# Experts' gates and ups as stationary operands, and VectorE steps with one operand from SBUF, in a linear-attention and mixture-of-experts layer

## The chip, the cores and the metric

The kernel runs on one core of a Trainium2 chip. The metric is the device time of one execution in microseconds (us). Matrix products run on TensorE (PE in the profile, its weight loads PEld); element-wise work runs on VectorE (DVE), ScalarE (ACT) and GpSimd (POOL). SyncE (SP) issues most transfers, POOL those that are indexed by row. Products land in PSUM; the kernel keeps everything else on the chip in SBUF.

## What is computed

A block on x of 4 batches x 1024 tokens x 256 channels, everything in fp32: x + attention(norm(x)) + experts(norm(x)).

```python
# attention, 16 heads of 16 channels
sq, sk = elu(q) + 1, elu(k) + 1
coarse = (sq @ M) / clip(sq @ z)                     # M, z: sums over 4 memories
fine   = sum_m softmax(mean n_f)[m] * (sq @ M_m) / clip(sq @ z_m)
prob   = sigmoid(relu(coarse @ eg_w1.T + eg_b1) @ eg_w2.T + eg_b2)
memory = prob * fine + (1 - prob) * coarse
local  = causal_linear_attention(q, k, v, chunk=128)
out    = (gate * memory + (1 - gate) * local) @ w_o.T
# experts: 8, of 176 inner channels, the best two of each token; one shared expert of 352
g = silu(x @ w_gate[e].T) * (x @ w_up[e].T)
y = sum_e cw[:, e] * (g @ w_down[e].T) + shared(x)
```

## The kernel before

**Stages.** The 4096 tokens are 32 tiles of 128. A first stage (to about 50 us) normalizes all of them, writes the normalized rows to a buffer `xns` in HBM and computes the values and the router's logits. Then the tokens are sorted by expert into 71 tiles of 128 slots, each tile with rows of one expert alone. From about 90 us on come 32 rounds, counted from 0, one for each token tile, and a tail. Each round does the attention of its token tile; rounds 2 to 29 also take a share of the projections, of the shared expert and of the 71 expert tiles. All is issued in an order written out by hand: every step is a unit with a weight, and `mix` merges the lists of a round in proportion to these weights. Each engine works through its own instructions in that order, and waits on semaphores where it needs another engine.

**A round of attention** (`attention_round`). `scores` (line 723) writes four masks' worth of products into the PSUM tile `quad`; VectorE masks them (`sT`, line 730). `turned(n-1)` (line 892) transposes `o` of the tile before, together with `coarse`. `output` multiplies it with `w_o` (`po`, lines 990 and 994). `memory` (line 838) reuses `quad`, once the masks have read it. `weigh` makes `rw` and `coarse` on VectorE (lines 848 to 853) and `cg` on POOL (line 860). `gate_hidden` forms the product `ph`, and VectorE adds the bias and reduces it to `z` (lines 917 and 919). `fine` makes `fm` in two VectorE steps (line 867); POOL makes `diff` of it in three steps (lines 878, 881, 882). `local` multiplies the masked scores with the values (`pn`, line 749). `gate_out(n-1)` makes `prob` on ScalarE and VectorE (lines 925 and 926) and `o = diff * prob + base` on VectorE (line 928). `back` (lines 765 and 771) forms `pb` in PSUM; VectorE makes `rden` of its denominators (lines 779 to 781) and `loc` (line 783). POOL adds `cg` to `loc` (line 789), which is `base` for the next round's `gate_out`. `loc` has one buffer. `update` adds to the running state (lines 818, 824, 829).

**An expert tile j.** `fetch_rows` gathers 128 rows of `xns` (POOL, line 1038). `fetch_weights` reads the expert's gates and ups (`wgu`) and downs (`wdn`) on SP. `expert_turn` transposes the hidden rows of tile j and the gathered rows of tile j+2 into one bank `pte`, and ScalarE copies it to `turned` (line 1077). `expert_hidden` multiplies: the turned rows are stationary, 352 columns of gates and ups move through, and `phe` has tokens on the partitions. ScalarE takes a tanh (line 1089) and VectorE two steps (lines 1090 and 1091). `expert_out` multiplies the turned hidden rows with `wdn` in two halves of 88 channels (`pye`, line 1097), ScalarE weighs the result (line 1101), and `put` adds it to the rows of `sums` in HBM (POOL, line 1106).

**PSUM.** `quad` takes four of the eight banks. All other products of the rounds take turns on four banks (`ps_r`, made by `bank`), in the order in which they are issued.

Of the kernel before, what the change touches and what calls it, by code (L numbers as in the profile page):

```python
# [8 lines left out]
FP = mybir.dt.float32  # L9
I32 = mybir.dt.int32  # L10
AF = mybir.ActivationFunctionType
ALU = mybir.AluOpType
AX = mybir.AxisListType

P = 128
NT = 4
TB = P * NT
EPS = 1e-6
# [4 lines left out]
def linear_attention_moe_kernel(  # L23
# [28 lines left out]
    nc = tc.nc  # L52
    T, H = x.shape
    S = T // B
    NH = memory_gate.shape[1]
    HD = H // NH
    NC = H // P
    HC = NH // NC
    NG = HC // 2
    NM = memories.shape[1]  # L60
    D1 = HD + 1
    CW = 32
    FR = E * F
    FT = w_gate.shape[1]
    FS = FT - FR
    NF = -(-FS // P)
    FH = F // 2
    assert FH * 2 == F and FH <= P and NC == 2 and NM == 4
    HID = eg_w1.shape[1]
    NBLK = T // TB  # L70
    NTT = T // P

    NST = 2 * NTT + E - 1
# [7 lines left out]
    const = ctx.enter_context(tc.tile_pool(name="const", bufs=1))  # L81
    io = ctx.enter_context(tc.tile_pool(name="io", bufs=NBLK))
    att = ctx.enter_context(tc.tile_pool(name="att", bufs=2))
    tmp = ctx.enter_context(tc.tile_pool(name="tmp", bufs=2))
    small = ctx.enter_context(tc.tile_pool(name="small", bufs=2))
    big = ctx.enter_context(tc.tile_pool(name="big", bufs=NBLK + 1))
    exw = ctx.enter_context(tc.tile_pool(name="exw", bufs=3))
    exp = ctx.enter_context(tc.tile_pool(name="exp", bufs=2))
    dram = ctx.enter_context(tc.tile_pool(name="dram", bufs=1, space=bass.MemoryType.DRAM))
# [5 lines left out]
    st = {}  # L95
    def bank(name):
        return ps_r.tile([P, 512], FP, tag="r", name=name)
# [48 lines left out]
    b1 = const.tile([P, HID], FP, tag="b1", name="b1")  # L146
# [27 lines left out]

    xns = dram.tile([T + P, H], FP, tag="xns", name="xns")
    sums = dram.tile([T + P, H], FP, tag="sums", name="sums")
    ident = const.tile([P, P], FP, tag="ident", name="ident")
    make_identity(nc, ident)
    ones = const.tile([P, P], FP, tag="ones", name="ones")
# [5 lines left out]
    for e in range(E):  # L185
# [5 lines left out]
        base=0, pattern=[[1, P]], channel_multiplier=-1,  # L191
# [53 lines left out]
    normx = const.tile([P, NC, NM, HC], FP, tag="normx", name="normx")  # L245
    alive = const.tile([P, NMN], FP, tag="alive", name="alive")

    hidden = [const.tile([P, FH + P], FP, tag=f"hidden{k}", name=f"hidden{k}") for k in range(2)]
    for t in hidden:
        nc.gpsimd.memset(t[:, F:], 0.0)  # L250
    ungate = const.tile([P, NH], FP, tag="ungate", name="ungate")
    gates = const.tile([P, H], FP, tag="gates", name="gates")

# [505 lines left out]
    def back(n):  # L759
        nT = st.pop(("nT", n))  # L760
        nq = NH // 4
        pb = bank(f"pb_{n}").rearrange("p (q t) -> p q t", q=nq)

        for q in range(nq):
            nc.tensor.matmul(
                pb[:, q, :], nT[:, q, :], ident,
                start=(q == 0), stop=False, is_transpose=True, skip_group_check=True,
            )
        blk, i, tok = at(n)
        for c in range(NC):  # L770
            nc.tensor.matmul(
                pb[:, 2 * c : 2 * c + 2, :].rearrange("p q (r k) -> p (q r) k", k=CW)[:, :, :D1],
                st["sqT", blk][:, c, tok],
                states[n % 2][:, c],
                start=False, stop=(c == NC - 1), skip_group_check=True,
            )
        pn3 = pb.rearrange("p q (r k) -> p (q r) k", k=CW)
        rden = small.tile([P, NH], FP, tag="rden", name=f"rden_{n}")
        nc.vector.tensor_scalar(rden, pn3[:, :, HD], EPS, None, ALU.max)
        nc.vector.reciprocal(rden, rden)  # L780
        nc.vector.tensor_mul(rden, rden, ungate)
        loc = tmp.tile([P, H], FP, tag="loc", name=f"loc_{n}", bufs=1)
        nc.vector.tensor_mul(  # L783
            loc.rearrange("p (h k) -> p h k", k=HD),
            pn3[:, :, :HD],
            rden[:, :, None].to_broadcast([P, NH, HD]),
        )

        nc.gpsimd.tensor_add(loc, loc, st["cg", n])
        st["base", n] = loc  # L790
# [117 lines left out]
    def gate_hidden(n):  # L908

        cT = st.pop(("cT", n))  # L910
        ph = bank(f"ph_{n}")
        for c in range(NC):
            nc.tensor.matmul(
                ph[:, :HID], cT[:, c, :], w1[:, c, :], start=(c == 0), stop=(c == NC - 1)
            )
        h1 = tmp.tile([P, HID], FP, tag="h1", name=f"h1_{n}")
        nc.vector.tensor_add(h1, ph[:, :HID], b1)  # L917
        z = small.tile([P, 1], FP, tag="z", name=f"z_{n}")
        nc.vector.scalar_tensor_tensor(h1, h1, 0.0, w2, ALU.max, ALU.mult, accum_out=z)
        st["z", n] = z  # L920

    def gate_out(n):

        prob = small.tile([P, 1], FP, tag="prob", name=f"prob_{n}")
        nc.scalar.activation(prob, st.pop(("z", n)), AF.Tanh, bias=b2, scale=0.5)
        nc.vector.tensor_scalar(prob, prob, 0.5, 0.5, ALU.mult, ALU.add)  # L926
        o = tmp.tile([P, H], FP, tag="o", name=f"o_{n}", bufs=1)
        nc.vector.scalar_tensor_tensor(  # L928
            o, st.pop(("diff", n)), prob, st.pop(("base", n)), ALU.mult, ALU.add
        )  # L930
        st["o", n] = o


    def shared_gate(blk, f):
# [99 lines left out]
    def fetch_rows(j):  # L1034
        if j >= NST:
            return
        xg = exp.tile([P, H], FP, tag="xg", name=f"xg_{j}", bufs=3)
        nc.gpsimd.indirect_dma_start(  # L1038
            out=xg,
            out_offset=None,  # L1040
            in_=xns,
            in_offset=bass.IndirectOffsetOnAxis(ap=islot[:, j : j + 1], axis=0),
        )
        st["xg", j] = xg

    def fetch_weights(j):
        if j >= NST:
            return
        e = nc.sync.value_load(owner[0:1, j : j + 1], min_val=0, max_val=(E - 1) * F)
        wgu = exw.tile([P, NC, 2, F], FP, tag="wgu", name=f"wgu_{j}")  # L1050
        for g, w in enumerate((w_gate, w_up)):
            nc.sync.dma_start(
                wgu[:, :, g, :],
                w[:, bass.ds(e, F)].rearrange("(k p) f -> p k f", p=P),
            )
        wdn = exw.tile([FH, 2, H], FP, tag="wdn", name=f"wdn_{j}")
        nc.sync.dma_start(
            wdn, w_down[bass.ds(e, F), :].rearrange("(f p) h -> p f h", p=FH)
        )
        st["weights", j] = wgu, wdn  # L1060

    def expert_turn(j):


        fetch_rows(j + 4)
        fetch_weights(j + 3)
        pt = bank(f"pte_{j}").rearrange("p (f t) -> p f t", t=P)
        lo, hi = (0 if j >= 0 else 2), (4 if j + 2 < NST else 2)
        if j >= 0:
            for f in range(2):  # L1070
                nc.tensor.transpose(pt[:, f, :], hidden[j % 2][:, f * FH : f * FH + P], ident)  # L1071
        if j + 2 < NST:
            xg = st.pop(("xg", j + 2))
            for c in range(NC):
                nc.tensor.transpose(pt[:, 2 + c, :], xg[:, c * P : (c + 1) * P], ident)  # L1075
        dst = exp.tile([P, 4, P], FP, tag="turned", name=f"turned_{j}")
        nc.scalar.copy(dst[:, lo:hi], pt[:, lo:hi])  # L1077
        st["hTe", j], st["xgT", j + 2] = dst[:, 0:2], dst[:, 2:4]

    def expert_hidden(j):  # L1080
        xgT, wgu = st.pop(("xgT", j)), st["weights", j][0]
        ph = bank(f"phe_{j}")
        for k in range(NC):
            nc.tensor.matmul(  # L1084
                ph[:, : 2 * F], xgT[:, k, :], wgu[:, k].rearrange("p g f -> p (g f)"),
                start=(k == 0), stop=(k == NC - 1),
            )
        th = hidden[j % 2][:, :F]
        nc.scalar.activation(th, ph[:, :F], AF.Tanh, scale=0.5)  # L1089
        nc.vector.scalar_tensor_tensor(th, th, 1.0, ph[:, :F], ALU.add, ALU.mult)  # L1090
        nc.vector.scalar_tensor_tensor(th, th, 0.5, ph[:, F : 2 * F], ALU.mult, ALU.mult)

    def expert_out(j):
        hT, wdn = st.pop(("hTe", j)), st.pop(("weights", j))[1]
        py = bank(f"pye_{j}")
        for f in range(2):
            nc.tensor.matmul(  # L1097
                py[:, :H], hT[:FH, f, :], wdn[:, f, :], start=(f == 0), stop=(f == 1)
            )
        y = exp.tile([P, H], FP, tag="y", name=f"y_{j}", bufs=3)  # L1100
        nc.scalar.activation(y, py[:, :H], AF.Copy, scale=wslot[:, j : j + 1])  # L1101
        st["y", j] = y
# [102 lines left out]
        return u  # L1205

    def experts():
        units = [(3000, lambda: None), (256, expert_turn, -2), (256, expert_turn, -1)]
        for j in range(NST + 1):
            if j < NST:  # L1210
                units += [(704, expert_hidden, j)]
            units += [(64, put, j - 2)] if j > 1 else []
            units += [(512, expert_out, j - 1)] if j > 0 else []
            units += [(512, expert_turn, j)] if j < NST else []
        return units + [(64, put, NST - 1)]

    def split(units, parts):
# [41 lines left out]
    for blk in range(NBLK):  # L1259
        rows = slice(blk * TB, (blk + 1) * TB)  # L1260
        nc.sync.dma_start(sums[rows, :], x[rows, :])


    def sorting():
# [128 lines left out]
```

## Time and profile before

| | |
|---|---|
| median of 3 runs | 688.77 us (687.68 to 692.53) |
| the profiled execution | 687.07 us |
| its span, first to last instruction | 685.4 us |
| mean granted clock of TensorE | 0.99 |
| VectorE / ScalarE / POOL busy | 454.8 / 267.1 / 386.8 us |
| DMA | 81.52 MB, 119 GB/s in the mean |

A row of the costliest groups gives line, engine and operation, what is written and read, the shape, the count, then the busy time in us and the mean duration in ns, and last the idle time of the engine before them with what ended it. A row of the list of waits gives who waited for whom, us in total, how often, and the longest in us. A row of the timeline gives start and duration in us. Matmuls overlap each other, so that the time from one start to the next says what one costs, and a weight load overlaps the matmul before it. An fp32 product appears as two matmuls over the same columns, a transpose as one.

### The profile page before, as it was taken

How to read it: one execution, taken by the hardware profiler on the slowest of the kernel's cores; microseconds unless marked ns; L12 is line 12 of the kernel's file. 1: busy time of each engine (PE TensorE's matmuls, PEld its weight loads, DVE VectorE, ACT ScalarE, POOL GpSimd, SP SyncE). 2: the span in 40 equal slices, each digit the busy share in tenths (PEclk: the TensorE clock that was granted, in tenths of full speed). 3: DMA queues.
4: the chain of work that ended last, by engine and by line, in shares of the span. 5: the costliest groups of instructions: out<-in, count | busy, mean ns of one | idle time of the engine just before them, and what ended most of it. 6: DMA issues, size and time to landing. Idle time of an engine off the chain costs nothing.

```text
span 685.4 us, 14244 instructions
## 1 busy us (share of the span) xinstructions
PE 646.1 (94%) x5084; PEld 461.9 (67%) x5084; DVE 454.8 (66%) x1198; ACT 267.1 (39%) x614; POOL 386.8 (56%) x424
## 2 busy tenths in 40 slices
PE   4999999899999899999999999999898999999896
PEld 3874565677777666676776767677676776667475
DVE  6838997666666657565756666666676566777672
ACT  3754644334444343334433333334343444334210
POOL 4300254556776735565565555566666567686575
PEclk9999999999999989999999999999999999999999
DMA  9683000436565623344453433345556466563384
GB/s 302 216 279 93 0 1 2 119 91 160 119 145 127 141 64 84 91 100 94 95 103 88 98 95 92 83 112 125 120 124 142 102 145 139 127 149 75 80 282 154
DMA packets 86483, 81.52 MB, mean 119 GB/s; under 512 B 7549, under 2 KB 84013, under 8 KB 86285
## 3 DMA queue, kind: packets, MB, share of 16 engines
q1 hardware_dynamic: 71085, 60.40, 30.6%
q0 software_dynamic: 13632, 18.62, 16.0%
q10 hardware_dynamic: 1696, 1.58, 0.7%
q8 instruction: 41, 0.67, 0.4%
q14 instruction: 29, 0.24, 0.1%
HBM read 62.62 MB, written 22.15 MB: 124 GB/s over the span
## 4 chain that ended last, share of the span: by engine, by line
PE 78%; DVE 14%; ACT 3%; issue 2%; POOL 1%; DMA 1%; DVEq 0%; ACTq 0%
PE phe L1084 13%; PE pye L1097 9%; PE po L990 6%; PE quad L723 5%; PE psu L953 5%; PE pv L396 4%; PE pg L939 4%; PE pn L749 4%; PE po L994 4%; PE quad L838 4%; PE pk L632 3%; PE pq L632 3%; PE pte L1071 2%; PE pt L892 2%; PE pte L1075 2%
## 5 line engine op out<-in xcount | busy, mean ns | idle before, releaser
L1106 POOL DMA_INDIRECT sums<-y,islot x71 | 113.3, 1596 | 70.3 <-DMA sums<-y,islot 18.8
L1084 PE MATMUL phe<-wgu,turned 128*128 128x352 f32 x276 | 97.5, 476 | 3.0 <-ACT turned L1077 2.2
L1090 DVE SCALAR_TENSOR_TENSOR hidden<-hidden,phe 128x176 f32<-128x176 f32 x71 | 23.8, 335 | 95.5 <-ACT hidden L1089 94.9
L730 DVE TENSOR_TENSOR sT<-quad,causal 128x512 f32<-128x512 f32 x128 | 80.5, 683 | 7.5 <-PE quad L723 7.1
L1038 POOL DMA_INDIRECT xg<-xns,islot x71 | 70.5, 993 | 18.7 <-issue 10.8
L1097 PE MATMUL pye<-wdn,turned 88*128 88x256 f32 x284 | 76.7, 393 | 2.5 <-issue 2.4
L860 POOL TENSOR_TENSOR cg<-coarse,gates 128x256 f32<-128x256 f32 x32 | 24.5, 765 | 95.5 <-DVE h L917 59.0
L1084 PEld LDWEIGHTS phe<-wgu,turned 128*128 128x128 f32 x276 | 48.5, 192 | 25.8 <-issue 6.4
L1097 PEld LDWEIGHTS pye<-wdn,turned 88*128 88x128 f32 x284 | 49.8, 190 | 16.4 <-issue 9.9
L1101 ACT ACTIVATE y<-pye,wslot 128x256 f32<-128x256 f32 x71 | 33.6, 473 | 64.0 <-PE pye L1097 64.0
L878 POOL TENSOR_TENSOR fm<-fm 128x512 f32<-128x512 f32 x32 | 44.1, 1379 | 20.0 <-DVE fm L867 12.4
L1077 ACT COPY turned<-pte 128x512 f32<-128x512 f32 (+1 forms) x71 | 41.1, 578 | 34.2 <-PE pte L1075 32.0
L1089 ACT ACTIVATE hidden<-phe 128x176 f32<-128x176 f32 x71 | 22.5, 317 | 78.6 <-PE phe L1084 76.5
L939 PE MATMUL pg<-xnT,wg 128*128 128x512 f32 (+1 forms) x96 | 45.7, 598 | 1.8 <-DVE loc L783 1.8
L990 PE MATMUL po<-wd,h 128*128 128x256 f32 (+1 forms) x192 | 47.2, 382 | 0.1
L953 PE MATMUL psu<-xnT,wu 128*128 128x512 f32 (+1 forms) x96 | 45.6, 597 | 0.0
L590 POOL TENSOR_TENSOR held<-ones,two 128x213 f32<-128x213 f32 (+1 forms) x22 | 15.3, 702 | 48.7 <-DVE ones L570 48.7
L867 DVE TENSOR_TENSOR fm<-quad,rw 128x512 f32<-128x512 f32 x64 | 42.0, 680 | 0.0
L848 DVE TENSOR_SCALAR rw<-quad 128x80 f32<-128x80 f32 x32 | 7.6, 239 | 49.3 <-PE quad L838 49.3
L990 PEld LDWEIGHTS po<-wd,h 128*128 128x128 f32 (+1 forms) x192 | 35.2, 191 | 6.3 <-ACT oc L902 0.8
L928 DVE SCALAR_TENSOR_TENSOR o<-diff,prob,loc 128x256 f32<-128x256 f32 x32 | 35.5, 1109 | 3.9 <-DVE prob L926 0.5
L749 PE MATMUL pn<-sT,va 128*32 128x128 f32 x1024 | 34.6, 276 | 0.3 <-ACT turned L1077 0.3
(210 smaller groups left out, 1389.0 us busy)
## 6 DMA issues: line engine op xcount, KB each, us to landing
wgu<-in_w_gate_dram SPq DMA_DIRECT2D x71, 176.0 KB
wgu<-in_w_up_dram SPq DMA_DIRECT2D x71, 176.0 KB
wdn<-in_w_down_dram SPq DMA_DIRECT2D x71, 176.0 KB
xns<-x SPq DMA_DIRECT2D x8, 512.0 KB
sums<-in_x_dram SPq DMA_DIRECT2D x8, 512.0 KB
x<-in_x_dram SPq DMA_DIRECT2D x7, 512.0 KB
part<-sums SPq DMA_DIRECT2D x12, 256.0 KB
out_dram<-acc SPq DMA_DIRECT2D x12, 256.0 KB
```

The costliest lines, as they stand in the source:

```text
L632: nc.tensor.matmul(pq, w[:, k, c * P : (c + 1) * P], xnT[:, k, :], start=(k == 0), stop=(k == NC - 1),)
L730: nc.vector.tensor_mul(sT, quad[:, g, :].rearrange("p (c t) -> p c t", t=P), causal[:, None, :].to_broadcast([P, NC * 2, P]),)
L749: nc.tensor.matmul(pn[CW * r : CW * (r + 1), q, :], wide[:, i, first : first + CW], st["sT", h // 2][:, c * 2 + h % 2, :], start=True, sto ...
L867: nc.vector.tensor_mul(fm[:, c].rearrange("p g m (r k) -> p g (m r) k", k=HD), quad[:, :, c * KM + KX + KN : (c + 1) * KM].rearrange("p g ...
L878: nc.gpsimd.tensor_add(fm[:, :, 0:2, :], fm[:, :, 0:2, :], fm[:, :, 2:4, :])
L939: nc.tensor.matmul(pg[:n, :], wg[:, k, f * P : f * P + n], xnT[:, k, :], start=(k == 0), stop=(k == NC - 1),)
L953: nc.tensor.matmul(pu[:n, :], wu[:, k, f * P : f * P + n], xnT[:, k, :], start=(k == 0), stop=(k == NC - 1),)
L990: nc.tensor.matmul(po[:, :H], st["h", blk, f][:k, tok], wd[:k, f, :], start=(f == 0), stop=False)
L1038: nc.gpsimd.indirect_dma_start(out=xg, out_offset=None, in_=xns, in_offset=bass.IndirectOffsetOnAxis(ap=islot[:, j : j + 1], axis=0),)
L1084: nc.tensor.matmul(ph[:, : 2 * F], xgT[:, k, :], wgu[:, k].rearrange("p g f -> p (g f)"), start=(k == 0), stop=(k == NC - 1),)
L1097: nc.tensor.matmul(py[:, :H], hT[:FH, f, :], wdn[:, f, :], start=(f == 0), stop=(f == 1))
L1106: nc.gpsimd.indirect_dma_start(out=sums, out_offset=bass.IndirectOffsetOnAxis(ap=islot[:, j : j + 1], axis=0), in_=st.pop(("y", j)), in_of ...
```

## The change

Experts: gates and ups become the stationary operands, the turned rows move, and `phe` has inner channels on the partitions, so that the hidden rows need no transpose. The 176 channels are split into 112 and 64. Three slices of columns are taken from `wgu`: 128 gates; the last 64 gates with the last 64 ups; and the first 112 ups. For this the ups of each expert are copied at the start into a buffer `ups` in HBM with their last 64 channels first. `wdn` is read with 112 partitions, and the second half of the last product takes 96 rows, 32 of which meet zeros in `hidden`.

VectorE: the denominators in `back` and the hidden row of `gate_hidden` stay in PSUM and are worked on in place. `gate_out` moves for tiles 0 to 28: ScalarE scales `prob` and `diff`, POOL adds `base`.

The order: a turn now fetches rows j+2 and weights j+1 for its own tile, and stands ahead of `expert_out(j-1)`; the units' weights follow.

```diff
-    FH = F // 2
+    FB = P // 2
+    FA = F - FB
...
+    ups = dram.tile([H, FR], FP, tag="ups", name="ups")
...
-    hidden = [const.tile([P, FH + P], FP, tag=f"hidden{k}", name=f"hidden{k}") for k in range(2)]
+    hidden = [const.tile([P, 2, P], FP, tag=f"hidden{k}", name=f"hidden{k}") for k in range(2)]
     for t in hidden:
-        nc.gpsimd.memset(t[:, F:], 0.0)
+        nc.gpsimd.memset(t, 0.0)
...
-        nc.vector.tensor_scalar(rden, pn3[:, :, HD], EPS, None, ALU.max)
-        nc.vector.reciprocal(rden, rden)
-        nc.vector.tensor_mul(rden, rden, ungate)
+        den = pn3[:, :, HD]
+        nc.vector.tensor_scalar(den, den, EPS, None, ALU.max)
+        nc.vector.reciprocal(den, den)
+        nc.vector.tensor_mul(rden, den, ungate)
...
-        h1 = tmp.tile([P, HID], FP, tag="h1", name=f"h1_{n}")
-        nc.vector.tensor_add(h1, ph[:, :HID], b1)
+        h1 = ph[:, :HID]
+        nc.vector.tensor_add(h1, h1, b1)
...
-        nc.vector.tensor_scalar(prob, prob, 0.5, 0.5, ALU.mult, ALU.add)
+        if n >= NTT - 3:
...
+            return
+        nc.scalar.activation(prob, prob, AF.Copy, bias=0.5, scale=0.5)
         o = tmp.tile([P, H], FP, tag="o", name=f"o_{n}", bufs=1)
-        nc.vector.scalar_tensor_tensor(
-            o, st.pop(("diff", n)), prob, st.pop(("base", n)), ALU.mult, ALU.add
-        )
+        nc.scalar.activation(o, st.pop(("diff", n)), AF.Copy, scale=prob)
         st["o", n] = o
+        nc.gpsimd.tensor_add(o, o, st.pop(("base", n)))
...
-        for g, w in enumerate((w_gate, w_up)):
+        for g, w in enumerate((w_gate, ups)):
...
-        wdn = exw.tile([FH, 2, H], FP, tag="wdn", name=f"wdn_{j}")
+        wdn = exw.tile([FA, 2, H], FP, tag="wdn", name=f"wdn_{j}")
         nc.sync.dma_start(
-            wdn, w_down[bass.ds(e, F), :].rearrange("(f p) h -> p f h", p=FH)
+            wdn, w_down[bass.ds(e, 2 * FA), :].rearrange("(f p) h -> p f h", p=FA)
         )
...
     def expert_turn(j):
-        fetch_rows(j + 4)
-        fetch_weights(j + 3)
...
+        fetch_rows(j + 2)
+        fetch_weights(j + 1)
+        pt = bank(f"pte_{j}").rearrange("p (c t) -> p c t", t=P)
+        xg = st.pop(("xg", j))
+        for c in range(NC):
+            nc.tensor.transpose(pt[:, c, :], xg[:, c * P : (c + 1) * P], ident)
+        xgT = exp.tile([P, NC, P], FP, tag="turned", name=f"turned_{j}")
+        nc.scalar.copy(xgT, pt[:, :NC])
...
-                ph[:, : 2 * F], xgT[:, k, :], wgu[:, k].rearrange("p g f -> p (g f)"),
...
+        for s, cols in enumerate((slice(0, P), slice(FA, FA + P), slice(F + FB, 2 * F))):
+            for k in range(NC):
+                nc.tensor.matmul(
+                    ph[: cols.stop - cols.start, s, :],
+                    wgu[:, k].rearrange("p g f -> p (g f)")[:, cols],
+                    xgT[:, k, :],
+                    start=(k == 0), stop=(k == NC - 1),
+                )
+        th = exp.tile([P, 2, P], FP, tag="th", name=f"the_{j}")
+        nc.scalar.activation(th, ph[:, :2], AF.Tanh, scale=0.5)
+        nc.vector.scalar_tensor_tensor(th, th, 1.0, ph[:, :2], ALU.add, ALU.mult)
+        h = hidden[j % 2]
+        nc.vector.scalar_tensor_tensor(
+            h[:FA, 0], th[:FA, 0], 0.5, ph[:FA, 2], ALU.mult, ALU.mult
+        )
+        nc.vector.scalar_tensor_tensor(
+            h[:FB, 1], th[:FB, 1], 0.5, ph[FB:, 1], ALU.mult, ALU.mult
+        )
...
-        for f in range(2):
+        for f, n in enumerate((FA, FB + 32)):
             nc.tensor.matmul(
-                py[:, :H], hT[:FH, f, :], wdn[:, f, :], start=(f == 0), stop=(f == 1)
+                py[:, :H], hT[:n, f, :], wdn[:n, f, :], start=(f == 0), stop=(f == 1)
             )
...
-        units = [(3000, lambda: None), (256, expert_turn, -2), (256, expert_turn, -1)]
+        units = [(3000, lambda: None), (256, expert_turn, 0), (256, expert_turn, 1)]
         for j in range(NST + 1):
-            if j < NST:
-                units += [(704, expert_hidden, j)]
+            units += [(768, expert_hidden, j)] if j < NST else []
             units += [(64, put, j - 2)] if j > 1 else []
+            units += [(256, expert_turn, j + 2)] if j + 2 < NST else []
             units += [(512, expert_out, j - 1)] if j > 0 else []
-            units += [(512, expert_turn, j)] if j < NST else []
...
+    for dst, src in ((slice(FB, F), slice(0, FA)), (slice(0, FB), slice(FA, F))):
+        nc.sync.dma_start(
+            ups.rearrange("h (e f) -> h e f", f=F)[:, :, dst],
+            w_up[:, :FR].rearrange("h (e f) -> h e f", f=F)[:, :, src],
+        )
```

More of the change, by code (lines that the diff above doesn't have):

```diff
@@ L66, in linear_attention_moe_kernel @@
     NF = -(-FS // P)
-    FH = F // 2
-    assert FH * 2 == F and FH <= P and NC == 2 and NM == 4
+    FB = P // 2
+    FA = F - FB
+    assert FA <= P and F >= P and NC == 2 and NM == 4
     HID = eg_w1.shape[1]
@@ L925, in gate_out @@
         nc.scalar.activation(prob, st.pop(("z", n)), AF.Tanh, bias=b2, scale=0.5)
-        nc.vector.tensor_scalar(prob, prob, 0.5, 0.5, ALU.mult, ALU.add)
+        if n >= NTT - 3:
+            nc.vector.tensor_scalar(prob, prob, 0.5, 0.5, ALU.mult, ALU.add)
+            o = tmp.tile([P, H], FP, tag="o", name=f"o_{n}", bufs=1)
+            nc.vector.scalar_tensor_tensor(
+                o, st.pop(("diff", n)), prob, st.pop(("base", n)), ALU.mult, ALU.add
+            )
+            st["o", n] = o
+            return
+        nc.scalar.activation(prob, prob, AF.Copy, bias=0.5, scale=0.5)
         o = tmp.tile([P, H], FP, tag="o", name=f"o_{n}", bufs=1)
-        nc.vector.scalar_tensor_tensor(
-            o, st.pop(("diff", n)), prob, st.pop(("base", n)), ALU.mult, ALU.add
-        )
+        nc.scalar.activation(o, st.pop(("diff", n)), AF.Copy, scale=prob)
         st["o", n] = o
+        nc.gpsimd.tensor_add(o, o, st.pop(("base", n)))
     def shared_gate(blk, f):
@@ L1062, in expert_turn @@
     def expert_turn(j):
-        fetch_rows(j + 4)
-        fetch_weights(j + 3)
-        pt = bank(f"pte_{j}").rearrange("p (f t) -> p f t", t=P)
-        lo, hi = (0 if j >= 0 else 2), (4 if j + 2 < NST else 2)
-        if j >= 0:
-            for f in range(2):
[L1071 to L1075, printed above, removed]
@@ L1076, in expert_turn @@
-        dst = exp.tile([P, 4, P], FP, tag="turned", name=f"turned_{j}")
-        nc.scalar.copy(dst[:, lo:hi], pt[:, lo:hi])
-        st["hTe", j], st["xgT", j + 2] = dst[:, 0:2], dst[:, 2:4]
+        fetch_rows(j + 2)
[5 more added lines that the diff above has]
+        xgT = exp.tile([P, NC, P], FP, tag="turned", name=f"turned_{j}")
@@ L1080, in expert_hidden @@
+        nc.scalar.copy(xgT, pt[:, :NC])
+        st["xgT", j] = xgT
     def expert_hidden(j):
         xgT, wgu = st.pop(("xgT", j)), st["weights", j][0]
-        ph = bank(f"phe_{j}")
-        for k in range(NC):
-            nc.tensor.matmul(
-                ph[:, : 2 * F], xgT[:, k, :], wgu[:, k].rearrange("p g f -> p (g f)"),
[L1086 to L1089, printed above, removed]
@@ L1090, in expert_hidden @@
-        nc.vector.scalar_tensor_tensor(th, th, 1.0, ph[:, :F], ALU.add, ALU.mult)
-        nc.vector.scalar_tensor_tensor(th, th, 0.5, ph[:, F : 2 * F], ALU.mult, ALU.mult)
+        ph = bank(f"phe_{j}").rearrange("p (s t) -> p s t", t=P)
+        for s, cols in enumerate((slice(0, P), slice(FA, FA + P), slice(F + FB, 2 * F))):
[6 more added lines that the diff above has]
+                )
@@ new lines, in expert_hidden @@
+        th = exp.tile([P, 2, P], FP, tag="th", name=f"the_{j}")
[5 more added lines that the diff above has]
+        )
+        nc.vector.scalar_tensor_tensor(
+            h[:FB, 1], th[:FB, 1], 0.5, ph[FB:, 1], ALU.mult, ALU.mult
+        )
+        st["hTe", j] = h
@@ L1095, in expert_out @@
         py = bank(f"pye_{j}")
-        for f in range(2):
+        for f, n in enumerate((FA, FB + 32)):
             nc.tensor.matmul(
-                py[:, :H], hT[:FH, f, :], wdn[:, f, :], start=(f == 0), stop=(f == 1)
+                py[:, :H], hT[:n, f, :], wdn[:n, f, :], start=(f == 0), stop=(f == 1)
             )
@@ L1261, in linear_attention_moe_kernel @@
         nc.sync.dma_start(sums[rows, :], x[rows, :])
+    for dst, src in ((slice(FB, F), slice(0, FA)), (slice(0, FB), slice(FA, F))):
+        nc.sync.dma_start(
+            ups.rearrange("h (e f) -> h e f", f=F)[:, :, dst],
+            w_up[:, :FR].rearrange("h (e f) -> h e f", f=F)[:, :, src],
+        )
     def sorting():
```

## The prediction

> **What bounds the kernel now.** I read the page's busy times first, then its chain of waits, then the groups by line, then the list of PE's waits, and last the timeline of one round.
>
> ```profile
> PE 646.1 (94%) x5084; PEld 461.9 (67%) x5084; DVE 454.8 (66%) x1198; ACT 267.1 (39%) x614; POOL 386.8 (56%) x424
> ...
> PE 78%; DVE 14%; ACT 3%; issue 2%; POOL 1%; DMA 1%; DVEq 0%; ACTq 0%
> ...
> L1084 PE MATMUL phe<-wgu,turned 128*128 128x352 f32 x276 | 97.5, 476 | 3.0 <-ACT turned L1077 2.2
> L1090 DVE SCALAR_TENSOR_TENSOR hidden<-hidden,phe 128x176 f32<-128x176 f32 x71 | 23.8, 335 | 95.5 <-ACT hidden L1089 94.9
> ...
> L928 DVE SCALAR_TENSOR_TENSOR o<-diff,prob,loc 128x256 f32<-128x256 f32 x32 | 35.5, 1109 | 3.9 <-DVE prob L926 0.5
> ```
>
> TensorE is busy 94% and carries 78% of the chain. VectorE has slack (454.8 of 685 us), so cheaper VectorE steps pay only where PE waits for one. PE's waits say how often that is:
>
> ```profile
> PE pt L892 <- DVE o L928: 2.2, 1, 2.2
> PE phe L1084 <- ACT turned L1077: 2.2, 8, 0.5
> PE pg L939 <- DVE loc L783: 1.8, 1, 1.8
> ...
> PE pte L1071 <- DVE loc L783: 1.1, 2, 0.6
> ...
> PE pt L892 <- DVE rden L779: 0.9, 1, 0.9
> ...
> PE pte L1071 <- DVE rden L779: 0.8, 1, 0.8
> ```
>
> The five on `o`, `loc`, `rden` come to 6.8 us; they are one chain, which one round shows (start, duration; POOL, VectorE, PE of round 11):
>
> ```profile
> 308.60 1.27 POOL L878 TENSOR_TENSOR fm<-fm 128x512 f32<-128x512 f32 x1 [0.82 <-DVE fm L867]
> 309.94 0.79 POOL L881 TENSOR_TENSOR diff<-fm 128x256 f32<-128x256 f32 x1
> 310.81 0.72 POOL L882 TENSOR_TENSOR diff<-diff,cg 128x256 f32<-128x256 f32 x1
> ...
> 307.83 0.68 DVE L867 TENSOR_TENSOR fm<-quad,rw 128x512 f32<-128x512 f32 x1
> ...
> 309.02 1.12 DVE L928 SCALAR_TENSOR_TENSOR o<-diff,prob,loc 128x256 f32<-128x256 f32 x1
> ...
> 310.80 0.42 DVE L783 TENSOR_TENSOR loc<-pb,rden 128x256 f32<-128x256 f32 x1
> ...
> 309.16 0.63 PE L771 MATMUL pb<-state,sqT 128*128 128x136 f32 x4
> 309.62 0.38 PE L1071 MATMUL pte<-ident,hidden 128*128 128x128 f32 x2
> 309.84 0.38 PE L1075 MATMUL pte<-ident,xg 128*128 128x128 f32 x2
> 310.06 0.63 PE L818 MATMUL pu<-va,sk 128*128 128x136 f32 x4
> ```
>
> The reader is to see three things. PE is paced by starts, not by durations: four 136-column matmuls take 309.62 - 309.16 = 0.46 us, four 128-column ones 0.44. `loc` ends at 311.22, that is 2.7 us after `fm` (308.51). And `pb`, which `loc` reads, lies in one of four rotating PSUM banks: PE can't start the fourth product behind `pb` before `loc` has ended.
>
> **The change part by part.**
>
> *PE's slots.* The two transposes of the hidden rows go: 71 tiles x 2 x 0.11 = 15.6 us. Four 352-column passes (1.18 us in most steps of the chain; 71 x 1.18 = 83.8) become twelve of 128 columns, each with its own weight load: 71 x 12 x 0.11 = 93.7. Together -5.7 us. Here a rule can be weighed. The row: 0.11 us for 128 columns with a 128-column load, 0.115 for 136. The Trainium skill (TensorE: Matmul & The Clock Gate, "Back-to-back issue gap") gives 81 ns as the sustained spacing at 128 columns. By it the twelve would cost 69.0 us and PE would gain 30; by the row 5.7. I take the row, since it is this kernel's own fp32 stream. From above: if each load showed in full (190 ns, the rows of PEld), the twelve would cost 162 us, 68 more. The 128-column rows beside it exclude nearly all of that; one exposed load per tile would be 71 x 0.11 = 7.8.
>
> *Waits of the gates' products.* `turned` is now the moving operand, made two tiles ahead without the hidden rows in it. I strike the row `phe <- turned`: -2.2.
>
> *VectorE's expert steps.* Two of 176 columns (335 and 337 ns) become 256, 128 and 128 columns. Between 335 ns at 176 and 679 ns at 512 columns (line 965) lie 1.02 ns a column: 417 + 286 + 286 = 989 ns, 317 more per tile, 22.5 us in all. The last step reads PSUM from partition 64. A rule speaks against this: VectorE: DVE Perf Modes, "Two Vector instructions with no wait between them", says that an instruction whose input starts in another group of 32 partitions than the last one from that memory is held until all before it have finished. Neighbours in this trace overlap by about 0.09 us (a step of 0.69 us from 306.64, the next from 307.24); losing that twice a tile is 0.18 us. No instruction of the trace shows the case. Bounds: 0 and 0.18; I take 0.18, which counts only where the steps stand before `fm`: eight rounds, 1.4 us.
>
> *Other VectorE steps.* `o` (1.109) and `prob` (0.147) leave for 29 of 32 rounds, 36 us. The step of line 919 takes 653 ns in the mean, but 0.23 where POOL is idle; with one PSUM operand I take 0.23. The `rden` product falls from 402 to about 220. All this is hidden by VectorE's idle third, except that `fm` ends 0.43 earlier.
>
> *ScalarE and POOL.* ScalarE: tanh over 256 columns 383 ns (between 317 and 595), `turned` 366 instead of 578, and 29 x (0.29 + 0.50) for `prob` and `o`: 13 us more on an engine at 39%. POOL gets 29 additions of 128x256 at 0.75: 22 us more. That is covered by its idle 44% as a load, but not as a position, which is next.
>
> *The added wait.* POOL takes `o + base` in order behind its three `fm`/`diff` steps, and `base` is the single `loc` buffer. So VectorE's next `loc` must wait for POOL. After `fm`: 0.09 + 1.27 + 0.79 + 0.72 + 0.75 with gaps = 3.85, then `loc` 0.42: it ends 4.3 us after `fm`, not 2.7. On VectorE `state`, the expert steps and the next masks queue behind it; PE waits for `pb`'s bank and for `o`. In the new order PE's fourth product comes sooner: behind `pb` often `pu` 0.46, `pte` 0.22, `pye` 0.86, scores 1.05 = 2.6 us (2.8 to 3.6 before). From the end of `memory`, PE needs the bank after 7.3 + 0.5 us in the ordinary rounds 3 to 7, 20 to 24 and 27 (0.5 is what rounds of before take over such a sum); `fm` ends at 3.8 (0.14 + 1.72 for `rw` and `coarse`, 0.6 for `h1`, 1.3), so `loc` ends at 8.1: 0.3 lost in each of 11, 3.3 us. In rounds 2, 9, 15, 17 and 25 the expert steps stand between the two `fm` and push the second one by 1.0 or more: 1.6 + 1.3 + 0.8 + 1.3 + 1.8 = 6.8. In rounds 11, 13 and 19 the steps between the two `fm` belong to a product that PE issues late: its end at about 5.7, 0.6 to the end of tanh, 1.05 of steps, 0.68 `fm` gives 8.0 instead of 3.8; `loc` ends at 12.3 against a bank wanted at 9.3: 3.0 each, 9.0. In the rest long projections lie in front: 0.3 in all. Sum 19.4, in place of the 6.8 of today.
>
> *Transfers.* SP issues two copies into `ups` (2.9 MB read and written) behind those of `sums`; the stage from 60 to 110 us has a DMA share of 0.00 to 0.01, and the first expert needs them at about 133. Without that cover the first tile would start late by the copy, a few us. `wdn` grows from 176 to 224 KB, 3.4 MB on 81.5 at a share under 0.6; PE waits for weights nowhere. Both cost nothing.
>
> *Sum:* -5.7 - 2.2 - 6.8 + 19.4 + 1.4 = +6.1 us. On the profiled execution (687.07) that is 693.2; it lies 1.7 under the median of the runs (688.77), on which it is 694.9.
>
> **The rivals.**
> 1. *Faster: POOL's addition stays covered.* Before, a round takes about 1 us more than PE's slots; if that slack takes up the wait, and `loc` is bound by PE as in most rounds now, only the gains remain: -5.7 - 2.2 and up to -6.8: 674 to 681, about 677. For it: PE's transpose of `o` comes 4 to 7 us after `fm` in most rounds of before. Against it: `pb`'s bank is wanted earlier than that. It decides at 2.6 us: if `loc` ends within that behind `pb`, PE doesn't notice.
> 2. *Much slower: the wait hits every round in full.* `loc` later by 1.6 us in 27 rounds with no slack is +44, less 14.7: about 718; with half of it, 704. VectorE standing still before `loc` delays the masks and with them `memory`, which needs their bank. For it: PE's work and the chain are nearly equal in length. Against: VectorE has 6 us idle a round.
> 3. *The loads show:* one a tile 7.8, all of them 68: 703 to 760. Against it speak the 0.11 us rows.
> 4. *VectorE's steps get no cheaper* (the contention is elsewhere): `fm` ends 0.43 later in some 19 waiting rounds, +8: 703.
>
> **How the numbers follow.** Forecast 0.50 (686 to 702), rival 1 0.20, rival 2 0.18, rivals 3 and 4 0.12. The time is 695. The range 677 to 710 leaves out half of rival 1 and the far ends of 2 and 3. Faster by over 1% (under 681.9) is rival 1 with little more: 0.19. Slower by over 1% (above 695.7) is just under half of the forecast (0.22) and nearly all of rivals 2 to 4: 0.48. The rest, 0.33, is within 1%, about what a measurement of this kernel can't tell from no change.
>
> **What would show it.** PE starts of the twelve passes 0.11 us apart; no more row for line 1071; a row of VectorE's `loc` waiting for POOL's `o`, with about 2 us a round; PE rows waiting for `loc` with some 15 to 20 us in all, most in rounds 11, 13 and 19; the three steps at about 0.42, 0.29 and 0.29. If `loc` waits for POOL and PE still has no rows for it, rival 1 was right; if PE's passes start 0.19 apart, rival 3.

## The result: 721.5 us, and the profile after

| | before | after |
|---|---|---|
| median of 4 runs each | 689.2 us (687.7 to 692.5) | 721.5 us (716.8 to 721.6) |
| ratio, 95% interval | | 1.045 (1.039 to 1.050) |
| the profiled execution's span | 685.4 us | 719.9 us |
| granted clock of TensorE | 0.990 | 0.974 |

The change costs 32 us. Here and below, runs over 1.5% above the fastest of the same kernel are left out, which for e3 leaves two runs of four.

First the busy times and the chain of waits on the page of the kernel after:

```profile
PE 658.4 (91%) x5510; PEld 498.3 (69%) x5510; DVE 427.7 (59%) x1211; ACT 275.5 (38%) x670; POOL 405.0 (56%) x453
...
PE 76%; DVE 10%; POOL 5%; issue 4%; ACT 4%; DMA 1%; POOLq 0%; DVEq 0%; ACTq 0%
```

VectorE is 27 us less busy than before, as meant, and POOL 18 us more. But PE is down to 91% of a longer span, and POOL, 1% of the chain before, now carries 5%. The groups that the change touched, on the same page:

```profile
L1095 PE MATMUL phe<-turned,wgu 128*128 128x128 f32 (+1 forms) x852 | 113.0, 284 | 3.0 <-issue 3.0
L1103 DVE SCALAR_TENSOR_TENSOR the<-the,phe 128x256 f32<-128x256 f32 x71 | 29.8, 420 | 127.6 <-ACT the L1102 112.5
L788 DVE TENSOR_TENSOR loc<-pb,rden 128x256 f32<-128x256 f32 x32 | 13.6, 425 | 51.9 <-POOL o L943 51.4
```

The steps are as cheap as forecast (420 ns against 417). `loc` waits for POOL's `o` for 51.4 us in all, 1.8 a round against "about 2". PE's waits, in the list of waits of the kernel after:

```profile
PE pte L1083 <- PE pu L823: 5.7, 13, 0.8
PE pg L951 <- DVE loc L788: 5.7, 1, 5.7
PE pye L1118 <- ACT turned L1085: 4.2, 9, 0.5
PE pye L1118 <- issue: 3.7, 2, 2.5
...
PE pu L823 <- DVE loc L788: 2.0, 1, 2.0
PE pt L897 <- POOL o L943: 1.8, 2, 1.6
```

The row of 5.7 us, once, is round 29. Its timeline in the kernel after (start, duration):

```profile
659.61 0.69 DVE L872 TENSOR_TENSOR fm<-quad,rw 128x512 f32<-128x512 f32 x1
...
660.45 0.63 PE L775 MATMUL pb<-state,sqT 128*128 128x136 f32 x4
...
660.91 1.03 PE L1118 MATMUL pye<-wdn,hidden 112*128 112x256 f32 x4
...
661.78 0.63 PE L823 MATMUL pu<-va,sk 128*128 128x136 f32 x4
...
662.35 1.57 POOL L1127 DMA_INDIRECT sums<-y,islot  x1 [2.21 <-issue]
...
663.38 1.83 POOL L883 TENSOR_TENSOR fm<-fm 128x512 f32<-128x512 f32 x1
665.29 0.72 POOL L886 TENSOR_TENSOR diff<-fm 128x256 f32<-128x256 f32 x1
666.09 0.72 POOL L887 TENSOR_TENSOR diff<-diff,cg 128x256 f32<-128x256 f32 x1
666.77 0.72 POOL L943 TENSOR_TENSOR o<-o,loc 128x256 f32<-128x256 f32 x1
667.52 0.42 DVE L788 TENSOR_TENSOR loc<-pb,rden 128x256 f32<-128x256 f32 x1 [5.72 <-POOL o L943]
...
668.10 3.75 PE L951 MATMUL pg<-xnT,wg 128*128 128x512 f32 x4 [5.68 <-DVE loc L788]
```

Follow it backwards. `pg` is PE's third product behind `pb` and lies in `pb`'s bank; it can't start before `loc` has read that bank. `loc` waits for POOL's `o`. And `o` is late because in POOL's queue an expert's scatter to HBM stands ahead of `fm`, which had been ready since 660.3. (Why POOL stood for 2.21 us before that scatter, the row doesn't say.) In before, `o` was VectorE's and did not stand in that queue. The second price follows at once: `pg` takes 3.75 us for what takes 1.88 at full clock. The same stretch in three equal windows (columns: PE, weight loads, VectorE, ScalarE, POOL, clock, DMA share, GB/s):

```profile
652.00:659.00 7.00, 7.00 (x79) 5.07 (x77) 5.83 (x17) 1.25 (x3) 2.75 (x3) 1.00 0.29 52
659.00:666.00 7.00, 3.41 (x24) 2.83 (x20) 1.88 (x6) 2.72 (x7) 4.72 (x5) 0.96 0.33 37
666.00:673.00 7.00, 4.90 (x36) 2.38 (x36) 1.36 (x3) 0.60 (x1) 4.51 (x6) 0.55 0.19 21
```

PE stands from 662.1 to 668.1, and from 665.5 to 672.3 its granted clock is halved (0.55 in the mean of the last window). The wait of 5.7 us has cost about 8: half of the 4.2 us in which PE works at half clock comes on top.

### Which bank PE waits for

The list of waits splits one cause over many rows, because it names the instruction that ended last, not the bank. So I read the bank of every product from the program built from each kernel. It shows that a product gets a bank whose last reader has already been *issued*: the four banks are no strict ring, as I had taken them to be ahead of the prediction. For each product that started late (by over 0.1 us against its usual spacing) and within 0.3 us of the end of the last reader of its bank, the delay is put down to the tile that held the bank. Products are counted from 130 us on. Beside it stands half the time at halved clock within the span, which is about what that clock costs. All in us:

```
kernel                          pb    phe    pte   other    all   clock   span
before                         7.9    1.2    4.0    30.1   43.1     6.8   685.4
after                         20.9   15.0    5.9    35.4   77.3    18.8   719.9
loc_twice        (e1)          2.6   14.7    5.9    40.7   64.0    13.7   703.3
o_on_VectorE     (e2)          2.4   22.2    6.2    33.6   64.4    15.4   706.1
experts_alone    (e3)          2.3   23.2    6.0    35.4   67.0    17.1   709.4
VectorE_alone    (e4)         26.6    0.6    3.8    34.9   65.9    18.8   719.9
PSUM_steps       (e5)          2.7    1.5    4.1    31.4   39.7     5.1   678.6
o_alone          (e6)         33.8    0.9    3.7    34.6   73.1    29.0   732.0
o_alone, loc twice (e7)        8.5    0.7    4.0    33.4   46.5    10.2   690.1
e2, out first    (e10)         3.3    4.5    0.0    36.9   44.6     8.5   685.0
e10, old costs   (e12)         2.2    4.4    0.4    31.7   38.6     6.8   677.3
o_alone, loc later (e13)       2.6    4.0    3.4    36.9   46.9     5.1   688.1
after, out first (e14)        33.7    4.6    0.0    37.7   76.0    25.6   732.3
after, loc later (e15)         0.0   13.1    0.3    41.0   54.3     5.1   688.4
```

After less before: +13.0 for `pb`'s bank, +13.8 for `phe`'s, +7.2 for the rest and +12.0 for the clock; PE's slots, the time that its matmuls take at their usual spacing, fall by 7.8 (5 to 11, as "usual" is taken). That is +38 against 34.5 in the spans; a wait inside a stretch of halved clock is counted in both columns.

### The profile page after: what moved, and what is told of

Its sections match the earlier page's. It is cut to its first block, busy times and chain, and to the rows that moved or that the text cites. A ratio compares the mean times of both kernels' runs of the same rounds, so it can differ in the third digit from the quotient of the medians.

```text
span 719.9 us, 15168 instructions
## 1 busy us (share of the span) xinstructions
PE 658.4 (91%) x5510; PEld 498.3 (69%) x5510; DVE 427.7 (59%) x1211; ACT 275.5 (38%) x670; POOL 405.0 (56%) x453
## 4 chain that ended last, share of the span: by engine, by line
PE 76%; DVE 10%; POOL 5%; issue 4%; ACT 4%; DMA 1%; POOLq 0%; DVEq 0%; ACTq 0%
PE phe L1095 13%; PE pye L1118 9%; PE po L1002 6%; PE psu L965 5%; PE quad L727 4%; PE pg L951 4%; PE pv L400 4%; PE pn L753 4%; PE po L1006 4%; PE quad L843 3%; PE pq L636 3%; PE pk L636 3%; PE pte L1083 2%; PE pt L897 2%; PE ph L918 2%
## 5 line engine op out<-in xcount | busy, mean ns | idle before, releaser
L1095 PEld LDWEIGHTS phe<-turned,wgu 128*128 128x128 f32 (+1 forms) x852 | 104.4, 192 | 19.3 <-issue 17.2
L1095 PE MATMUL phe<-turned,wgu 128*128 128x128 f32 (+1 forms) x852 | 113.0, 284 | 3.0 <-issue 3.0
L1103 DVE SCALAR_TENSOR_TENSOR the<-the,phe 128x256 f32<-128x256 f32 x71 | 29.8, 420 | 127.6 <-ACT the L1102 112.5
L1118 PE MATMUL pye<-wdn,hidden 112*128 112x256 f32 (+1 forms) x284 | 79.8, 404 | 11.8 <-ACT turned L1085 4.2
L1118 PEld LDWEIGHTS pye<-wdn,hidden 112*128 112x128 f32 (+1 forms) x284 | 49.8, 193 | 26.1 <-issue 7.4
L883 POOL TENSOR_TENSOR fm<-fm 128x512 f32<-128x512 f32 x32 | 41.3, 1292 | 32.2 <-DVE fm L872 32.1
L1102 ACT ACTIVATE the<-phe 128x256 f32<-128x256 f32 x71 | 27.1, 381 | 81.7 <-PE phe L1095 75.6
L788 DVE TENSOR_TENSOR loc<-pb,rden 128x256 f32<-128x256 f32 x32 | 13.6, 425 | 51.9 <-POOL o L943 51.4
L1085 ACT COPY turned<-pte 128x256 f32<-128x256 f32 x71 | 26.5, 373 | 37.7 <-PE pte L1083 36.5
L1083 PE MATMUL pte<-ident,xg 128*128 128x128 f32 x142 | 28.9, 285 | 8.3 <-PE pu L823 5.7
```

The costliest lines, as they stand in the source:

```text
L1083: nc.tensor.transpose(pt[:, c, :], xg[:, c * P : (c + 1) * P], ident)
L1095: nc.tensor.matmul(ph[: cols.stop - cols.start, s, :], wgu[:, k].rearrange("p g f -> p (g f)")[:, cols], xgT[:, k, :], start=(k == 0), sto ...
L1118: nc.tensor.matmul(py[:, :H], hT[:n, f, :], wdn[:n, f, :], start=(f == 0), stop=(f == 1))
```

## The experiments

The expectations below were written one batch at a time, ahead of the runs. Those on banks by name (K, Q, B) were argued from the list of waits; the table above was made when all runs were there.

**e1: two buffers for loc, so that loc needn't wait for POOL.**

```diff
-        loc = tmp.tile([P, H], FP, tag="loc", name=f"loc_{n}", bufs=1)
+        loc = tmp.tile([P, H], FP, tag="loc", name=f"loc_{n}", bufs=2)
```

> The changed kernel with two buffers for loc, so that VectorE need not wait for POOL's addition o + base before it writes the next loc; POOL still does the addition. Theory W (the wait of loc for POOL, with the PSUM banks that VectorE holds behind it, is the loss): the 51 us of VectorE waiting go, and the time falls from 721 to 690 to 698. Theory X (the new layout of the experts is the loss: longer steps, more weight loads, lower clock): little changes, 714 to 721. Theory O (PE waits for o itself, which comes late from POOL): VectorE's wait goes, PE's rows wait for POOL's o instead, 708 to 718.

702.3 us, 1.020 (1.015 to 1.026): 19 of the 32 us are back, not all. The table says what stays: `pb` fell from 20.9 to 2.6, `phe` kept its 14.7.

**e2: o's two steps back on VectorE**, the lines of before in `gate_out`, all else as after.

> The changed kernel with prob and o on VectorE again in all rounds; the experts' layout and the steps in PSUM stay. W and O: loc no longer follows POOL, 683 to 692, a little faster than before by the 6 to 8 us of PE's slots. X: 712 to 720.

709.8 us, 1.032 (1.027 to 1.037). `loc` waits for POOL no more, and still 21 us are lost. So the experts' part costs something by itself.

**e3: before, with the experts' part alone** (layout, `ups`, order of the units); `back`, `gate_hidden` and `gate_out` as before.

> The kernel before with the experts' layout and their order alone; rden, h1, prob and o as before. W and O: 683 to 692 (PE's slots say -6 to -8). X: 712 to 720, the whole loss.

711.1 and 715.7 us, 1.036 of before's 688.8 in the same batch, though PE's slots are fewer. (The ratio on record, 1.050 with 1.040 to 1.060, is above both runs; I go by the runs.) So the experts' part alone loses some 25 us. One round of it (timeline of that kernel):

```profile
514.73 1.59 PE L1087 MATMUL phe<-turned,wgu 128*128 128x128 f32 x12
...
516.18 2.29 DVE L932 SCALAR_TENSOR_TENSOR o<-diff,prob,loc 128x256 f32<-128x256 f32 x1
...
516.36 0.38 ACT L1094 ACTIVATE the<-phe 128x256 f32<-128x256 f32 x1 [0.71 <-PE phe L1087]
...
517.06 0.63 PE L822 MATMUL pu<-va,sk 128*128 128x136 f32 x4
...
518.40 0.41 DVE L1095 SCALAR_TENSOR_TENSOR the<-the,phe 128x256 f32<-128x256 f32 x1
518.85 0.29 DVE L1097 SCALAR_TENSOR_TENSOR hidden<-the,phe 112x128 f32<-112x128 f32 x1
519.15 0.29 DVE L1100 SCALAR_TENSOR_TENSOR hidden<-the,phe 64x128 f32<-64x128 f32 x1
...
519.54 0.41 PE L1075 MATMUL pte<-ident,xg 128*128 128x128 f32 x2 [1.85 <-issue]
...
520.41 2.08 PE L1110 MATMUL pye<-wdn,hidden 112*128 112x256 f32 x4 [0.46 <-ACT turned L1077]
```

`pte` is the third product behind `phe` and lies in its bank. The three steps that read `phe` stand behind `o` on VectorE, which takes 2.29 us here while POOL works too, and end at 519.44; `pte` starts at 519.54. The list has only "issue" for it; the bank says what it was. Then `pye` takes 2.08 us instead of 1.03: halved clock again.

**e4: before, with VectorE's part alone** (denominators and bias sum in PSUM, `o` on ScalarE and POOL).

> The kernel before with VectorE's part alone: rden and h1 in PSUM, prob and o on ScalarE and POOL for tiles 0 to 28; the experts as before. W and O: most of the loss without the gain of PE's slots, 710 to 728. X: 684 to 692.

724.0 us, 1.056 (1.048 to 1.063). The two halves alone cost some 25 and 35 us, and both together 32. e5 and e6 divide this half further.

**e5: before, with the two steps in PSUM alone** (the diff's hunks in `back` and `gate_hidden`).

> Before, with only two of VectorE's steps changed: the clamped denominator and its reciprocal stay in PSUM, and so does the bias sum h1; o's two steps stay on VectorE and the experts stay as before. Theory W (the added loss of VectorE's part is loc waiting for POOL's o): 684-692, no loss. Theory D (it is a bank held longer because a step now writes PSUM): over 705. A theory in which the steps themselves are cheaper and on the path: below 682.

681.7 us, 0.993 (0.991 to 0.996): a small gain. `loc` and `ph`'s steps end earlier, and `pb`'s bank costs 2.7 instead of 7.9 us.

**e6: before, with o's move alone** (the hunk in `gate_out`).

> Before, with only o's two steps moved to ScalarE and POOL. Theory W (loc waits for POOL's o): all of the 35 us that the run with VectorE's whole part lost, so 712-728, with a row 'loc <- POOL o' of some 50 us. Theory D: 684-695.

730.4 us, 1.062 (1.054 to 1.071). The move of `o` is the whole loss of e4 and more. Its list of waits has, on VectorE:

```profile
DVE loc L783 <- POOL o L938: 58.3, 28, 4.4
```

**e7: e6 with two buffers for loc.**

> Before with o's two steps moved to ScalarE and POOL, and two buffers for loc, so that the next round's loc step needn't wait for POOL's addition. Theory W (the 43 us that the move alone cost are loc's wait, with the queue of VectorE and the banks behind it): 685-697, and no row of loc waiting for POOL's o. Theory P (o comes later from the loaded POOL, and its readers, the transposes of o, are late): 710-730.

690.9 us, 1.008 (1.006 to 1.011). One buffer was 40 of the 43 us. What is left, a later `o` among it, is some 5 us.

**e9: e3 with `expert_out` ahead of `expert_turn`**, the order in which before had them:

```diff
-            units += [(256, expert_turn, j + 2)] if j + 2 < NST else []
             units += [(512, expert_out, j - 1)] if j > 0 else []
+            units += [(256, expert_turn, j + 2)] if j + 2 < NST else []
```

> Before with the experts' new layout alone, and expert_out placed ahead of expert_turn in the order of a round, as before had it, so that the turn's product isn't the third behind phe. Theory K (the loss of the experts' part is TensorE waiting for phe's bank, which the turn wants while VectorE's three steps still queue, and the clock halved after it): 690-705, and the waits at pte gone. Theory L (the layout's passes, their 256-column sources or their spacing, cost it themselves): no better than 711.

694.0 us, 1.010 (1.000 to 1.020); by the count of the table, 4.4 us at `phe`'s bank and none at `pte`'s. **e10: the same order in e2.**

> After with o's two steps back on VectorE and expert_out ahead of expert_turn. It differs from the run with o on VectorE (709.8) by the order alone. Theory K: 685-700. Theory L: 705-715.

687.3 us, 1.002 (0.998 to 1.005): 22 us less than e2, by the order alone. `phe`'s bank fell from 22.2 to 4.5, `pte`'s from 6.2 to 0.

**e12: e10 with the planner's costs of before** (704 for `expert_hidden`, 512 for `expert_turn`), so that the units fall where before had most of them.

> After with o's steps on VectorE, expert_out ahead of expert_turn, and the planner's costs of the expert units as in before (704 and 512 in place of 768 and 256), so that most of them fall where before had them. The run with the same order and the new costs gave 687.3. If what is left against the 681.7 of before with the two PSUM steps is the places of the units: 674-681. If it is the layout itself: 685-690.

678.6 us, 0.989 (0.986 to 0.993): faster than both kernels, and the lowest time of the study. Its page:

```profile
PE 642.1 (95%) x5510; PEld 490.3 (72%) x5510; DVE 467.9 (69%) x1269; ACT 256.7 (38%) x612; POOL 386.7 (57%) x424
...
PE 83%; DVE 11%; ACT 2%; issue 1%; DMA 1%; POOL 1%; DVEq 0%; ACTq 0%
```

VectorE does 40 us more here than in after, and the kernel is 43 us faster. PE carries 83% of the chain, 76% in after.

**e11 and e14: after with out first, with two and with one buffer for loc.**

> After with two loc buffers and expert_out ahead of expert_turn. Two loc buffers alone gave 702, from 721; the order alone gave 22 us in the kernel with o on VectorE. Theory WK (two separate causes, whose prices add): 676-688. Theory S (they share the same waits, so the second brings little): 695-703.

> After with expert_out ahead of expert_turn and nothing else: o on POOL, one buffer for loc. Two loc buffers with this order gave 689, the old order with one buffer 721. Theory WK (the two prices add): 697-706. Theory S (each wait alone costs most of it, since TensorE has to be late only once in a round): 712-728.

e11: 689.0 us, 1.008 (1.005 to 1.010), between WK and S; by the same count, 1.5 us at `pb`'s bank and 2.2 at `phe`'s. e14: 733.2 us, 1.065 (1.060 to 1.071), which neither theory had: mending the order *alone* makes after 12 us slower. The table shows why the two prices don't add. With the order mended, `phe` costs 4.6 instead of 15.0, and `pb` 33.7 instead of 20.9. I read it so: a PE that has already waited for `phe`'s bank comes later to `pb`'s, and has less to wait there. No run tests this. `pb`'s bank is also held longer in e14: in rounds 4 to 6 and 20 to 24, 6.2 to 6.8 us from the first matmul of `pb` to the end of `loc`, against 3.7 to 5.5 in after; and other products follow in it.

**e13: e6 with loc later**: rden's steps and `loc` are issued behind `update`.

```diff
-        pn3 = pb.rearrange("p q (r k) -> p (q r) k", k=CW)
+        st["pb", n] = pb.rearrange("p q (r k) -> p (q r) k", k=CW)
+
+    def local_out(n):
+        pn3 = st.pop(("pb", n))
...
         u += unit(64, gate_out, n - 1) + unit(528, back, n) + unit(300, update, n)
+        u += unit(0, local_out, n)
```

> Before with o's two steps on ScalarE and POOL and one buffer for loc, as in the run that took 730, but the three steps of rden and loc's step are emitted behind the round's update, so that the multiply of pu, and in some rounds one expert's step or a projection's, stand ahead of loc on VectorE. Theory Q (TensorE waits for the banks of steps that queue behind the waiting loc: pu, phe, pq): 700-715. Theory B (it waits for pb's own bank, as my prediction's added wait had it: the fourth product behind pb): pb is held as long or longer, so 728-740.

691.9 us, 1.006 (1.004 to 1.009): 38 us back from one shift. **e15: the same edit in after.**

> After with one edit: rden's three steps and loc's step emitted behind the round's update. o stays on POOL, loc has one buffer, the experts' order is after's. In the kernel with o's move alone the same edit took 730 to 692. Theory Q (what loc's wait costs after is the queue behind loc): what is left is the order's price, so 700-712, as the run with o on VectorE (709.8). Theory B (pb's own bank): 718 or more.

693.1 us, 1.011 (1.008 to 1.013). Here is the trap of this study. The times of e13 and e15 lie nearer to Q, below the range of both, but the reasoning under both expectations was wrong: I took it that the fourth product would still lie in `pb`'s bank. It doesn't. Since `loc` is issued later, the products in between get other banks; from round 2 on, `pb`'s bank is used again by the fifth to seventh product in e15, by the second to fifth (mostly the fourth) in after. The delay at `pb` falls from 20.9 to 0.0 us, and in neither after nor e6 was a late product one that lay in `pu`'s or `pq`'s bank, as Q would have it. So B, PE waiting for `pb`'s own bank, is what the banks show. In e15's timeline of round 29 `pg` lies in a bank that `pye` had left, and starts 4.4 us before `loc`:

```profile
634.25 0.69 DVE L875 TENSOR_TENSOR fm<-quad,rw 128x512 f32<-128x512 f32 x1
...
636.40 0.63 PE L826 MATMUL pu<-va,sk 128*128 128x136 f32 x4
637.12 1.98 PE L954 MATMUL pg<-xnT,wg 128*128 128x512 f32 x4
...
641.48 0.42 DVE L791 TENSOR_TENSOR loc<-pb,rden 128x256 f32<-128x256 f32 x1 [2.71 <-POOL o L946]
```

POOL's scatter is as late there as in after; nobody on PE minds. VectorE still waits for `o`, but less:

```profile
DVE loc L791 <- POOL o L946: 23.0, 17, 2.7
```

**e16: e12 with loc later.**

> The fastest so far (o on VectorE, expert_out ahead of expert_turn, the planner's costs of before: 678.6) with rden and loc emitted behind the update. No loc waits for POOL there, so theory Q gives only what state and the experts' steps gain from standing ahead of four steps of 1.0 us: 674-679. If the later base of o (loc's addition on POOL) then holds o and its transposes: 680-686.

683.7 us, 0.997 (0.994 to 1.000), 5 us slower than e12. Its profiled span is 678.0, near e12's 677.3: `pb`'s bank costs 0.8 us against 2.1 there, but `phe`'s 8.3 against 4.2. Most of its runs were slower than the one profiled, and at a lower granted clock: 679.5 to 680.5 us at 0.995, 686.1 to 686.6 at 0.988. Why its clock differs so much from run to run is open.

## Why the prediction was wrong

The time, 721.5, lies above the range. By the terms of its sum:

| term | predicted | measured |
|---|---|---|
| PE's slots | -5.7 | -7.8 |
| old waits on o, loc, rden gone, added wait at `pb`'s bank | -6.8 + 19.4 = +12.6 | 20.9 - 7.9 = +13.0 |
| expert steps and their bank (`phe`) | +1.4 | +13.8 |
| wait for `turned`, now `pte`'s bank | -2.2 | +1.9 |
| other waits | 0 | +5.3 |
| halved clock | not in the sum | +12.0 |
| sum | +6.1 | +38 (spans: +34.5) |

The other waits and those at `pte`'s bank, +7.2 in all, I have not traced to a step of the prediction; their cause stays open.

**Two steps of the sum failed. The first is the one on VectorE's expert steps,** put at +1.4 us where `phe`'s bank took 13.8. It worked out the steps rightly (417, 286 and 286 ns; the trace has 420, 287, 290), let them count only where they stand before `fm`, and left the rest to VectorE's idle third. But an idle third is no cover for a bank. Twelve passes and three steps hold `phe`'s bank 3.09 us from its first matmul (median), 2.54 before. And the new order brings the next product of that bank sooner: without the wait, it would have started within 3.1 us of `phe` in 26 of the 71 tiles of after, in 8 of before and in 5 of e10. In 16 tiles of after it is `pte`, a product of only 0.22 us, that waits: 9.8 of the 15.0 us. I had asked which product wants the bank next for `pb` alone. e3 shows this price without POOL's part, e10 and e9 show it go when only the order is put back.

**The added wait was right in kind, and its sum was luck.** The bank cost 20.9 us, forecast 19.4, but in other rounds. The eleven ordinary rounds lost 4.5 us (forecast 3.3) and rounds 2, 9, 15, 17 and 25 lost 3.6 (6.8). Rounds 11, 13 and 19 lost 1.0 (9.0): in each, PE had already waited 0.7 us for `phe`'s bank just before, and the bank was used again only by the fifth product. All the rest, put at 0.3, lost 11.7. Of that round 29 lost 5.8, by a scatter in POOL's queue that I had not put ahead of `o`: I had named POOL's position as the question and then listed only its three `fm`/`diff` steps. "Fourth product behind `pb`" holds for 16 of the 30 rounds from round 2 on; in the others it is the second, third or fifth.

**The second step that failed: the clock was put at nothing,** where it took 12.0 us. Before had 13.7 us at half clock within its span, after 37.5. Of the nine gaps of 1.3 us or more between PE's starts from 130 us on in after, seven (1.49 to 5.96 us) are followed within 3.4 us of their start by a stretch of 3.4 or 6.8 us at half clock. Two (1.65 and 2.14 us) are not. After is the extreme case. In all 17 traces, counting the gaps that begin at full clock, such a stretch begins within 5.2 us of the start of all 20 gaps of 3 us or more, of 35 of the 59 from 2 to 3 us, and of 15 of the 56 from 1.3 to 2 us. The Trainium skill (TensorE: Matmul & The Clock Gate, "Why this matters for your kernels") advises against idle gaps of more than about 3 us; these traces agree, and shorter ones were often enough. So in this kernel a few long waits cost more than many short ones of the same sum. That the clock follows from the waits is read from the traces; no change to a kernel moved the clock alone. What the clock costs shows in runs of one and the same kernel: 30 runs of before in one batch reach from 682.1 us at 0.997 to 691.4 at 0.988, and fall by about 7 us for each 0.01 of clock.

**Rivals.** Rival 2 had 718 us, near the result, but for another reason: its +44 was `loc`'s wait in every round, where `pb`'s bank took 13. Rival 3 (weight loads show) fell: the passes are 0.112 us apart in the median. Rival 1's mechanism was possible: in e15 and e7 POOL's addition is covered. Rival 4 fell: the product for `rden` went from 402 to 174 ns in the mean and the second step on `ph` from 653 to 232, and in e5 the steps in PSUM gained 0.7%, some 4.5 us. The copies into `ups` and the larger `wdn` cost nothing that shows: `memory` of round 2, beside the first expert tile, starts at 134.9 us, at 136.6 before. The rule on VectorE's held steps, which the prediction weighed at 0 to 0.18 us a tile, shows: the step that reads PSUM from partition 64 starts 14 ns after the end of the one before it in all 71 tiles, and most steps behind it 31 ns after its end. In before, steps behind the last expert step started some 82 ns ahead of its end. That is about 0.2 us a tile, near the 0.18 taken.

## What to carry to other kernels

Ask of each PSUM bank, not of each engine: how long is it held from the first matmul to the last reader, and which product is issued into it next. A step moved to another engine may be free in load and still hold a bank, because a single buffer chains it to that engine's whole queue; a second buffer, or issuing the reader behind the products that follow, took 19 to 40 us off here (e1, e7, e13, e15). Test parts separately and together: two losses of this kind hid in each other, and mending one of them alone (the order, e14) made the kernel slower.

## What the runs showed of the hardware

- Stretches at half clock lasted 3.4, 6.8 or (e6, e14) 10.2 us. One followed every gap of 3 us or more between PE's starts (20 of 20 in 17 traces), and about one in four of those from 1.3 to 2 us (15 of 56).
- Runs of one kernel differ by their granted clock: before took 682.1 us at 0.997 and 691.4 at 0.988, e16 679.5 at 0.995 and 689.7 at 0.983.
- One VectorE step, `o`, took 0.48 to 2.15 us in before, 1.11 in the mean. In e3 it took 2.29 while POOL worked too.
- A VectorE step that reads PSUM from partition 64 behind one that reads it from partition 0 did not overlap it: it started 14 ns after its end (after, 71 of 71). Neighbours that both read from partition 0, neither of them the other's result, overlap by some 82 ns.
